# Key and value weights loaded as whole rows, first group's steps of unequal length, a normalization and some weight sums issued at other places

## The chip, the cores and the metric

The kernel runs on one core of a Trainium2 chip. The metric is the device time of one execution in microseconds (us); where several runs are shown, their median is given. Engines are named TensorE (PE in the profile, with PEld for its weight loads), VectorE (DVE), ScalarE (ACT), GpSimd (POOL) and SyncE (SP, which here only issues DMAs).

## The reference

A cross-attention block with a feed-forward block behind it, all in fp32, for 16 sequences of 128 tokens with 1024 features:

```python
x = x + xattn(layernorm(x), ctx, ctx, Wq, bq, Wk, bk, Wv, bv, Wo, bo)
x = x + ffn(layernorm(x), kernel, scale)

# xattn: 32 query heads of 32 features, 8 key/value heads, each shared by 4 query heads
Q = query @ Wq + bq            # 1024 x 1024
K = key @ Wk + bk              # 1024 x 256
V = value @ Wv + bv            # 1024 x 256
w = softmax(Q K^T / sqrt(32))  # per head, 128 x 128
y = w V
return y @ Wo + bo             # 1024 x 1024

# ffn: the last fifth of the features is weighted by -4; kernel holds zeros and ones
return scale * (concat(x[..., :819], -4 * x[..., 819:]) @ kernel)
```

The context is key and value at once, also 16 x 128 x 1024.

## The kernel before, in words

Two sequences make a group, so there are eight groups (`grp` 0 to 7). A group needs its context turned so that features lie on partitions (`cT`), keys (`prep_k`) and values (`prep_v`) from it, its normalized x turned in the same way (`prep_x`), queries (`prep_q`), attention in four steps, the output projection (`out_proj`) and the feed-forward product (`ffn`). The kernel is written so that TensorE always has dense products between the small products of attention: while group `grp` is in its four attention steps, the output projection and feed-forward of group `grp - 1` and the preparation of group `grp + 1` fill the spaces.

The order of all instructions is set by hand, by the class `Stream`. It has a model clock `now`, a queue of generators and a list of events. `piece` takes the next bit of dense work from the queue and adds its modelled length to `now`; `later(us, fn)` puts a call at a model time; `run(until)` alternates pieces with the events that are due. The model clock only orders the program: on the chip each engine takes its own instructions in program order and waits on semaphores. `mixed(dense, light, skip, every)` takes one item of `light` after every so many items of `dense`, and what is left of `light` at the end; `once(fn)` is a generator with one item of length zero; `spread(gen, us, then)` takes one step of a generator every `us`.

Attention is done in a step for each sequence and half of the heads (`attend(b, a, length)`). A step begins with 32 products of scores (`sc`, L513); at 0.7, 3.1, 5.5 and 7.9 us after them one of four blocks of heads gets its maximum on VectorE (`negm`, L525) and its exponentials on ScalarE (`p`, L529); 2.3 us later VectorE divides it (L541); and `length / 2 - 3.0` after the exponentials' event TensorE turns it (`tpp`, L546) and ScalarE copies it (`pt`, L548). At the end of the step come the products with the values (`av`, L556). `length` is 17.4 in the first group, 24.0 in groups 1 to 5 and 22.0 in group 6. PSUM tiles of `tpp`, `tp_x` (L310), `tp_f` (L646) and `av` share one pool of two buffers.

Queries and the output projection are computed with seven instead of eight block products (`seven`); for that, sums of blocks of Wq and Wo are made once by VectorE in group 0 (`combine`, L704), stored to DRAM and fetched again like the other pieces of weights through a ring of eight buffers (`fetch`, L218). `sums_of_wo` starts the sums of Wo's first half; those of the second half are started in `sums_of_wq` when Wq's second half is done. Partial results of the projection are added to the residual by VectorE straight from PSUM (L621), after which the accumulation goes on in the same PSUM tile.

The feed-forward product is made in two passes of fp32r, with a high and a low part of the turned, normalized x: `ffn_transpose` turns four chunks at a time (`tp_f`, L646), ScalarE rounds them to the high part (`x2h`, L648) and VectorE takes the difference (`x2l`, L649), after which the PSUM buffer is free.

`load_ctx` brings one sequence of context as four DMAs, each into 32 partitions: partition k * 32 + r holds rows r, r + 32, r + 64 and r + 96 of columns k * 256 to k * 256 + 255. `turn_ctx` (L319) then turns blocks of 32 x 32 on VectorE, four instructions for a group (a sequence and half of the features each). In the kernel before, chunk c of `cT` holds on partition k * 32 + f the feature k * 256 + c * 32 + f, and `load_by_quadrants` brings Wv and Wk in the same order, as four DMAs of 256 KB into 32 partitions each, alternating between SP's and ScalarE's queue.

`get_x(b, us)` loads a sequence's x (L167) and puts its normalization (`norm_x`: L276, L280, L282, the power on GpSimd at L284, L285) at `us` later. Loaded and normalized x (`xn`) and the normalized input of the feed-forward block (`x2n`) share three buffers. Residual x is loaded by `load_residual` (L172) and gets bo added by GpSimd (L178).

Of the kernel before, what the change touches and what calls it, by code (L numbers as in the profile page):

```python
# [17 lines left out]
P = 128  # L18
# [48 lines left out]
def mixed(dense, light, skip=0, every=1):  # L67


    for n, us in enumerate(dense):  # L70
        yield us
        if n >= skip and (n - skip) % every == 0:
            yield next(light, 0.0)
    yield from light


def once(fn, *args):
    fn(*args)
    yield 0.0
# [3 lines left out]
def kernel(  # L83
# [26 lines left out]
    GB = 2  # L110
# [38 lines left out]
    NB = P // 32  # L149

    def load_ctx(b, queues=(nc.sync,)):
        c_t = work.tile([P, NB, NC, 32], FP, tag="ctx", name=f"ctx{b}", bufs=2)
        src = key_value[b].rearrange("(t r) (k c f) -> k r t (c f)", r=32, k=NB, c=NC)
        for k in range(NB):
            dst = c_t[k * 32 : (k + 1) * 32].rearrange("r t c f -> r t (c f)")
            queues[k % len(queues)].dma_start(out=dst, in_=src[k])
        cs[b] = c_t

    def load_by_quadrants(dst, w, queues):
        src = w.rearrange("(k c f) n -> k f c n", k=NB, f=32)  # L160
        for k in range(NB):
            queues[k % len(queues)].dma_start(out=dst[k * 32 : (k + 1) * 32], in_=src[k])

    def load_x(b):

# [16 lines left out]

    two = (nc.sync, nc.scalar)
    load_ctx(0, two)
    load_by_quadrants(wv_sb, Wv, two)
    load_ctx(1, two)
    load_by_quadrants(wk_sb, Wk, two)
    load_x(0)
    load_x(1)
    nc.gpsimd.dma_start(out=bkT, in_=bk)  # L190
# [123 lines left out]
    def turn_ctx(b, h):  # L314
        grp, j = b // GB, b % GB
        if (grp, h) not in cTs:
            cTs[grp, h] = work.tile([P, HC, T], FP, tag="tT", name=f"cT{grp}_{h}", bufs=3)
        src = cs.pop(b) if h == 1 else cs[b]
        nc.vector.transpose(  # L319
            cTs[grp, h][:, :, j * S : (j + 1) * S].rearrange("p c (t n) -> p t c n", t=NB),  # L320
            src[:, :, h * HC : (h + 1) * HC],
        )

    def prep_ctx(grp, *us):
# [388 lines left out]
    def spread(gen, us, then=lambda: None):  # L713


        def step():
            if next(gen, "end") != "end":
                stream.later(us, step)
            else:
                then()  # L720

        stream.later(us, step)
# [14 lines left out]
    with tc.manual_schedule():  # L737
        stream = Stream()

        at_q = {}  # L740
        for k in range(2):
            for o in range(2):
                for r in range(2):
                    at_q[r, o, k] = want(lambda r=r, o=o, k=k: q_block(r, o, k))
        qs, os = {1: prep_q(1)}, {}
        for grp in range(NGRP):
            os[grp] = out_proj(grp)
            if grp + 2 < NGRP:
                qs[grp + 2] = prep_q(grp + 2)
        for _ in range(RING):  # L750
            fetch()
        o_parts = [load_o_part(0)]

        def plain(a):
            return prep_q_plain(a, {(r, k): at_q[r, a, k] for r in range(2) for k in range(2)})

        for j in range(GB):
            for h in range(2):
                turn_ctx(j, h)
            stream.add(prep_v(0, [j]))  # L760
        stream.add(prep_k(0))
        for j in range(GB):
            load_ctx(GB + j)
        stream.run(0.0, lambda: len(stream.queue) > 1)
        nc.vector.tensor_scalar_mul(bqs, bqT, scale)
        for j in range(GB):
            norm_x(j)

        def sums_of_wo():
            def then():  # L770
                o_parts.append(load_o_part(1))
                for j in range(GB):
                    load_x(GB + j)
                load_ffn()

            stream.later(4.0, lambda: spread(combine("o", 0, o_parts[0]), 1.5, then))

        stream.add(prep_x(0, 0), prep_x(0, 1), once(sums_of_wo), plain(0))
        stream.run(0.0, lambda: stream.queue)

        def get_x(b, us):
            load_x(b)
            stream.later(us, lambda: norm_x(b))

        def get_ctx(grp):
            if grp < NGRP:
                for j in range(GB):
                    load_ctx(grp * GB + j)

        def residuals(grp):  # L790
            for j in range(GB):
                load_residual(grp * GB + j, 1.0 if grp == 0 else 4.0)

        def sums_of_wq(k):
            def then():
                for _ in range(4):
                    fetch()
                if k == 1:
                    spread(combine("o", 1, o_parts[1]), 2.5)

            spread(combine("q", k, {(r, o): pieces[at_q[r, o, k]] for r, o in BLOCKS}), 1.5, then)

        def between(gen, n, fn, *args):

            for i, us in enumerate(gen):
                yield us
                if i + 1 == n:
                    fn(*args)

        for grp in range(NGRP):  # L810
            b0, b1, nxt = grp * GB, grp * GB + 1, grp + 1
            p0, p1 = b0 - 2, b0 - 1
            first, more = grp == 0, nxt < NGRP
            last = grp == NGRP - 1
            length = 17.4 if first else 24.0 if grp < NGRP - 2 else 22.0
            if first:
                stream.add(
                    once(prep_ctx, nxt, 12.5, 13.5),
                    between(plain(1), 9, sums_of_wq, 0),
                    once(sums_of_wq, 1),  # L820
                    once(turn_ctx, nxt * GB, 1),
                    once(turn_ctx, nxt * GB + 1, 1),
                    once(norm_x, nxt * GB),
                    prep_k(nxt),
                    once(get_ctx, nxt + 1),
                    once(norm_x, nxt * GB + 1),
                    prep_v(nxt),
                    prep_x(nxt, 0),
                    prep_x(nxt, 1),
                    once(convert_ffn),  # L830
                    between(qs[nxt], 40, residuals, grp),
                )
            elif more:
                stream.add(
                    once(get_x, nxt * GB, 14.0),
                    once(prep_ctx, nxt, 3.7, 8.0, 13.0, 18.0),
                    os[grp - 1],
                    once(get_ctx, nxt + 1),
                    prep_k(nxt),
                    mixed(prep_v(nxt), chain(ffn_transpose(p0), ffn_transpose(p1)), 1, 2),  # L840
                    once(get_x, nxt * GB + 1, 5.0),
                )
                if nxt < NGRP - 1:
                    stream.add(ffn(p0), mixed(ffn(p1), prep_x(nxt, 0), 12))
                else:
                    stream.add(mixed(ffn(p0), prep_x(nxt, 0), 14))
                stream.add(once(residuals, grp), prep_x(nxt, 1), qs[nxt])
            else:
                stream.add(
                    os[grp - 1],  # L850
                    mixed(ffn(p1 - 2), ffn_transpose(p0), 10, 2),
                    once(load_residual, b0, 2.0),
                    mixed(ffn(p0), ffn_transpose(p1), 8, 2),
                    once(load_residual, b1, 2.0),
                )
            if not more:
                for q in range(2 * NA):
                    b, a = grp * GB + q % GB, q // GB
                    start = stream.now
                    pts = attend(b, a, 15.0)  # L860
                    stream.later(15.0, lambda b=b, a=a, pts=pts: weighted(b, a, pts) or 1.0)
                    stream.run(start + 12.0)
                stream.drain()
                break
            for q in range(2 * NA):
                b, a = grp * GB + q % GB, q // GB
                start = stream.now
                pts = attend(b, a, length)
                if q == 2 * NA - 1:
                    stream.run(start + length - 2.0, lambda: stream.queue)  # L870
                else:
                    stream.run(start + length - 2.0)
                stream.run(stream.now, lambda: None in pts)
                weighted(b, a, pts)
                stream.now += 1.0
        stream.add(
            os[NGRP - 1],
            mixed(ffn(B - 3), ffn_transpose(B - 2), 10, 2),
            mixed(ffn(B - 2), ffn_transpose(B - 1), 8, 2),
            ffn(B - 1),  # L880
        )
        stream.drain()
# [49 lines left out]
```

## Time and profile before

| | us |
|---|---|
| median of 3 runs | 819.83 (819.57 to 819.86) |
| the profiled execution's own time | 817.83 |
| its span | 816.1 |
| TensorE busy | 789.8 (97%) |
| VectorE busy | 459.9 (56%) |
| ScalarE busy | 332.7 (41%) |
| first matmul starts | 12.29 |

Times within the profile count from the start of the span. In a timeline row the columns are: start, length, engine, line and operation, output and inputs with their shapes, number of instructions merged into the row, and in brackets how long the engine had been idle before it and what ended that. In a row of windows they are: the stretch, its length, busy time and number of instructions of each engine, the granted TensorE clock, the share of the DMA engines and the GB/s moved. Groups 1 to 5 follow one another at a distance of 97.5 us (their k products start at 153.3, 250.8, 348.4, 445.9 and 543.4).

### The profile page before, as it was taken

The page shows a single profiled execution, that of the slowest core. Times are in us where ns is not written, and L with a number is a line of the kernel's source. Part 1 is how long each engine was busy: PE and PEld are TensorE (multiplying, and loading weights), DVE is VectorE, ACT ScalarE, POOL GpSimd, SP SyncE. Part 2 cuts the span into 40 slices and gives each one's busy share as a digit, 9 for nine tenths or more (in the row PEclk, how much of TensorE's full clock was granted, in tenths as well). Part 3 has the DMA queues.
Part 4 walks back from the last instruction along what each step waited for, and adds up shares of the span by engine and source line. Part 5 has one row for each costly group of instructions (what it writes and reads, how often), then busy time and mean ns, then how long its engine had stood idle before and what let it go on. Part 6 is the DMA issues. An engine that isn't in the chain of part 4 may idle for free.

```text
span 816.1 us, 13885 instructions
## 1 busy us (share of the span) xinstructions
PE 789.8 (97%) x5216; PEld 593.4 (73%) x5216; DVE 459.9 (56%) x862; ACT 332.7 (41%) x1281; POOL 69.6 (9%) x109
## 2 busy tenths in 40 slices
PE   3997999999999999999999999999999999999998
PEld 3886884678947797488965889568894779756556
DVE  1369748554475554755456454765348565467442
ACT  0243854444334443345333544344434454366200
POOL 1000003002000020000300002000200002000300
PEclk9999999999999999999999999999999999999999
DMA  9999598715885178741887328780578307761511
GB/s 202 357 319 317 198 399 326 210 52 182 273 269 164 43 238 274 262 130 44 286 269 253 80 103 280 276 242 29 179 262 281 132 27 274 246 215 69 195 62 77
DMA packets 81075, 165.14 MB, mean 202 GB/s; under 512 B 5969, under 2 KB 42833, under 8 KB 81009
## 3 DMA queue, kind: packets, MB, share of 16 engines
q1 hardware_dynamic: 79200, 162.55, 59.6%
q10 hardware_dynamic: 1664, 1.57, 1.1%
q8 instruction: 41, 0.67, 0.3%
q0 software_dynamic: 144, 0.14, 0.1%
q14 instruction: 26, 0.20, 0.1%
HBM read 147.46 MB, written 16.78 MB: 201 GB/s over the span
## 4 chain that ended last, share of the span: by engine, by line
PE 86%; DMA 6%; DVE 3%; issue 2%; SPq 1%; ACT 1%; POOL 0%; ACTq 0%; DVEq 0%; POOLq 0%
PE o_u L607 14%; PE f L293 14%; PE q_u L396 12%; PE o_v L607 7%; PE tpp L546 6%; PE q_v L396 6%; PE k L293 5%; PE v L293 5%; PE sc L513 4%; PE av L556 4%; PE o_c L607 3%; PE q_c L396 3%; DMA wo<-in_L_xattn_Wo_dram 2%; PE tp_f L646 2%; PE tp_x L310 1%
## 5 line engine op out<-in xcount | busy, mean ns | idle before, releaser
L529 ACT ACTIVATE p<-sc,negm 128x128 f32<-128x128 f32 x512 | 181.1, 369 | 155.9 <-DVE negm L525 82.3
L548 ACT COPY pt<-tpp 128x512 f32<-128x512 f32 x128 | 74.8, 590 | 117.1 <-PE tpp L546 116.6
L525 DVE TENSOR_REDUCE negm<-sc 128x4 f32<-128x512 f32 x128 | 87.3, 683 | 39.8 <-PE sc L513 39.8
L293 PE MATMUL f<-wf_sb,x2l 128*128 128x512 f32 x256 | 106.0, 414 | 0.0
L529 ACT ACTIVATION_READ_ACCUMULATOR p<-sc,negm 128x1 f32 x512 | 105.8, 207 | 0.0
L293 PE MATMUL f<-wf_sb,x2h 128*128 128x512 f32 x256 | 101.2, 396 | 0.0
L541 DVE TENSOR_TENSOR p<-p,inv 128x512 f32<-128x512 f32 x128 | 88.6, 692 | 4.4
L546 PE MATMUL tpp<-ident,p 128*128 128x128 f32 x512 | 76.7, 273 | 6.3 <-DVE p L541 4.0
L546 PEld LDWEIGHTS tpp<-ident,p 128*128 128x128 f32 x512 | 61.7, 141 | 28.1 <-issue 20.0
L396 PE MATMUL q_u<-t,piece 128*128 128x128 f32 x672 | 81.2, 276 | 0.0
L396 PEld LDWEIGHTS q_u<-t,piece 128*128 128x128 f32 x672 | 78.0, 192 | 0.2 <-DMA piece<-q 0.2
L293 PE MATMUL v<-wv_sb,cT 128*128 128x256 f32 x256 | 62.6, 387 | 12.3 <-DMA wv_sb<-in_L_xattn_Wv_dram 12.3
L178 POOL TENSOR_TENSOR x<-x,bo_b 128x256 f32<-128x256 f32 x64 | 48.8, 795 | 180.2 <-DMA x<-in_x_dram 160.1
L293 PEld LDWEIGHTS v<-wv_sb,cT 128*128 128x128 f32 x256 | 47.5, 195 | 17.7 <-issue 12.3
L607 PE MATMUL o_u<-piece,yT 128*128 128x512 f32 x128 | 59.1, 603 | 0.0
L607 PE MATMUL o_u<-piece,s 128*128 128x512 f32 x128 | 59.0, 594 | 0.0
L607 PE MATMUL o_v<-piece,s 128*128 128x512 f32 x128 | 59.0, 594 | 0.0
L293 PE MATMUL k<-cT,wk_sb 128*128 128x256 f32 x256 | 57.0, 380 | 0.0
L293 PEld LDWEIGHTS f<-wf_sb,x2l 128*128 128x128 f32 x256 | 48.1, 188 | 11.4 <-issue 1.1
L293 PEld LDWEIGHTS f<-wf_sb,x2h 128*128 128x128 f32 x256 | 48.3, 189 | 10.0 <-issue 0.5
L293 PEld LDWEIGHTS k<-cT,wk_sb 128*128 128x128 f32 x256 | 48.5, 190 | 9.0 <-issue 2.6
L564 ACT COPY yT<-av 128x512 f32<-128x512 f32 x32 | 18.7, 585 | 88.0 <-PE av L556 88.0
(77 smaller groups left out, 949.8 us busy)
## 6 DMA issues: line engine op xcount, KB each, us to landing
piece<-o SPq DMA_DIRECT2D x64, 512.0 KB, 4.4
piece<-q SPq DMA_DIRECT2D x56, 512.0 KB, 4.4
piece<-in_L_xattn_Wq_dram SPq DMA_DIRECT2D x50, 512.0 KB, 4.8
piece<-in_L_xattn_Wo_dram SPq DMA_DIRECT2D x48, 512.0 KB, 4.5
xn<-in_x_dram SPq DMA_DIRECT2D x16, 512.0 KB, 5.4
x<-in_x_dram SPq DMA_DIRECT2D x16, 512.0 KB, 4.9
ctx<-in_ctx_dram SPq DMA_DIRECT2D x60, 128.0 KB, 5.9
out_dram<-x SPq DMA_DIRECT2D x15, 512.0 KB, 2.7
```

Of the source, the lines that this page charges most:

```text
L178: lambda cut=cut: nc.gpsimd.tensor_add(x_t[:, cut], x_t[:, cut], bo_b[:, cut]) and None,
L293: nc.tensor.matmul(mm, lhsT=lhsT, rhs=rhs, start=k == 0, stop=k == n - 1)
L396: nc.tensor.matmul(mm if part is None else mm[:, part], lhsT=lhsT, rhs=rhs, start=start and n == k == 0, stop=k == len(some) - 1, skip_gro ...
L513: nc.tensor.matmul(tiles[i][:, g], lhsT=qT[rows, g], rhs=kT[rows, a, cols], start=True, stop=True,)
L525: nc.vector.tensor_reduce(negm, tile_, AX.X, ALU.max, negate=True)
L529: nc.scalar.activation(p[:, g], tile_[:, g], AF.Exp, bias=negm[:, g : g + 1], accum_out=total[:, g : g + 1],)
L541: nc.vector.tensor_mul(p, p, inv.unsqueeze(2).to_broadcast([P, NG, S]))
L546: nc.tensor.transpose(tp[:, g], p[:, g], ident)
L548: nc.scalar.copy(pt, tp)
L556: nc.tensor.matmul(mm[i * HD : (i + 1) * HD], lhsT=vs[b][:, h * HD : (h + 1) * HD], rhs=pts[i], start=True, stop=True,)
L564: nc.scalar.copy(yTs[b, a], mm)
L607: nc.tensor.matmul(mm, lhsT=lhsT[:, 2 * k + c], rhs=w[:, c], start=start and k == c == 0, stop=k == c == 1, skip_group_check=True,)
```

## The change

Four things are changed together.

1. Chunk c of the turned context now holds on partition p the feature p * 8 + c. Wv and Wk are therefore loaded with eight whole rows to a partition, each as one DMA into 128 partitions on SP's queue. The DMAs of the context stay as they are (the same bytes go to the same places); only its transposes read every eighth word instead of 32 neighbouring ones.
2. In group 0 the four attention steps get the lengths 17.4, 22.4, 16.0 and 14.0 instead of four times 17.4.
3. The sums of Wo's second half start 8 us later on the model clock, and their steps are 3.0 apart instead of 2.5; the first sum thus comes at 11 instead of 2.5 us, the stores at 23 instead of 12.5.
4. In groups 1 to 6 the loading of the next group's second x stands between the transposes of the two feed-forward inputs, as an item of `mixed`, instead of behind both.

```diff
     def load_ctx(b, queues=(nc.sync,)):
-        c_t = work.tile([P, NB, NC, 32], FP, tag="ctx", name=f"ctx{b}", bufs=2)
-        src = key_value[b].rearrange("(t r) (k c f) -> k r t (c f)", r=32, k=NB, c=NC)
+        c_t = work.tile([P, NB, 32, NC], FP, tag="ctx", name=f"ctx{b}", bufs=2)
+        src = key_value[b].rearrange("(t r) (k n) -> k r t n", r=32, k=NB)
         for k in range(NB):
-            dst = c_t[k * 32 : (k + 1) * 32].rearrange("r t c f -> r t (c f)")
+            dst = c_t[k * 32 : (k + 1) * 32].rearrange("r t f c -> r t (f c)")
             queues[k % len(queues)].dma_start(out=dst, in_=src[k])
         cs[b] = c_t
-
-    def load_by_quadrants(dst, w, queues):
-        src = w.rearrange("(k c f) n -> k f c n", k=NB, f=32)
-        for k in range(NB):
-            queues[k % len(queues)].dma_start(out=dst[k * 32 : (k + 1) * 32], in_=src[k])
...
     load_ctx(0, two)
-    load_by_quadrants(wv_sb, Wv, two)
+    nc.sync.dma_start(out=wv_sb, in_=Wv.rearrange("(p c) n -> p c n", p=P))
     load_ctx(1, two)
-    load_by_quadrants(wk_sb, Wk, two)
+    nc.sync.dma_start(out=wk_sb, in_=Wk.rearrange("(p c) n -> p c n", p=P))
...
             cTs[grp, h][:, :, j * S : (j + 1) * S].rearrange("p c (t n) -> p t c n", t=NB),
-            src[:, :, h * HC : (h + 1) * HC],
+            src[:, :, :, h * HC : (h + 1) * HC].rearrange("p t f c -> p t c f"),
...
                 if k == 1:
-                    spread(combine("o", 1, o_parts[1]), 2.5)
+                    stream.later(8.0, lambda: spread(combine("o", 1, o_parts[1]), 3.0))
...
-            length = 17.4 if first else 24.0 if grp < NGRP - 2 else 22.0
+            length = 24.0 if grp < NGRP - 2 else 22.0
...
-                    mixed(prep_v(nxt), chain(ffn_transpose(p0), ffn_transpose(p1)), 1, 2),
-                    once(get_x, nxt * GB + 1, 5.0),
+                    mixed(
+                        prep_v(nxt),
+                        chain(
+                            ffn_transpose(p0),
+                            once(get_x, nxt * GB + 1, 5.0),
+                            ffn_transpose(p1),
+                        ),
+                        1,
+                        2,
+                    ),
...
                 start = stream.now
+                if first:
+
+                    length = (17.4, 22.4, 16.0, 14.0)[q]
                 pts = attend(b, a, length)
```

## Prediction

> **What bounds the kernel now.** I read the page first, then TensorE's timeline for its pauses, then VectorE's timeline around each pause, then DMA rates by window.
>
> ```profile
> span 816.1 us, 13885 instructions
> PE 789.8 (97%) x5216; PEld 593.4 (73%) x5216; DVE 459.9 (56%) x862; ACT 332.7 (41%) x1281; POOL 69.6 (9%) x109
> 12.29 8.64 PE L293 MATMUL v<-wv_sb,cT 128*128 128x256 f32 x32 [12.29 <-DMA wv_sb<-in_L_xattn_Wv_dram]
> 46.64 7.17 PE L293 MATMUL q<-xT,piece 128*128 128x256 f32 x32 [1.04 <-DVE qT L387]
> 72.45 0.63 PE L546 MATMUL tpp<-ident,p 128*128 128x128 f32 x4 [0.77 <-ACT p L529]
> 76.27 0.63 PE L546 MATMUL tpp<-ident,p 128*128 128x128 f32 x4 [0.60 <-DVE p L541]
> 81.99 0.63 PE L546 MATMUL tpp<-ident,p 128*128 128x128 f32 x4 [3.37 <-DVE p L541]
> 669.13 0.66 PE L310 MATMUL tp_x<-ident,xn 128*128 128x128 f32 x4 [0.71 <-ACT pt L548]
> 671.13 1.06 PE L310 MATMUL tp_x<-ident,xn 128*128 128x128 f32 x8 [0.88 <-DVE inv L540]
> ```
>
> TensorE is the bound: besides the first 12.29 us its only sizeable pauses are those above and 1.37 us at 749.7. From 103 to 668 us it never stops, and groups 1 to 5 repeat every 97.5 us. So the change can gain only in the first 103 us and near 670; between them any new wait is paid in full.
>
> ```profile
> 2.00:12.00 10.00, 0.00 (x0) 0.00 (x0) 1.30 (x2) 0.00 (x0) 1.89 (x5) 1.00 1.10 204
> 19.00:22.00 3.00, 3.00 (x15) 2.65 (x15) 1.03 (x4) 0.00 (x0) 0.00 (x0) 1.00 1.02 407
> 40.00:44.00 4.00, 3.68 (x18) 2.92 (x17) 0.90 (x3) 0.37 (x1) 0.00 (x0) 1.00 1.08 195
> 60.87 1.30 DVE L319 STREAM_TRANSPOSE cT<-ctx 128x512 f32<-128x512 f32 x2
> 64.72 1.30 DVE L319 STREAM_TRANSPOSE cT<-ctx 128x512 f32<-128x512 f32 x2
> 81.16 0.69 DVE L541 TENSOR_TENSOR p<-p,inv 128x512 f32<-128x512 f32 x1
> ```
>
> The last figure of a window is GB/s. Loads into 32 partitions run at about 200 (weights and context from 2 us; context alone from 40 us, through SP only, so the second queue isn't the cause); loads into 128 partitions (x, from 19 us) at 407.
>
> **The change part by part** (gains negative).
>
> *Weights in whole rows.* Wv leaves its 32-partition form. From the first packets at 2.0 us: context 0, 0.52 MB at 204 GB/s, 2.6 us; Wv, 1.05 MB at 407, 2.6 us; context 1's half from ScalarE's queue and bv_b interleave, 0.3 to 1.6 us; 0.3 us to landing. That is 7.8 to 9.1, and I take 8.5. The first v matmul then starts near 8.6, not 12.29: -3.7. SP gives up two issues for Wv and two for Wk (0.46 us each where the queue was free) and takes one for each, which I put at 0.33 to 0.92 (bo_b's issue into 128 partitions took 0.33); ScalarE's queue loses four. None of them is on the path, since the data take longer. Next in line is context 1, some 2 us behind Wv plus its transposes, about 12 to 13; v of batch 0 covers it (first seven matmul records at the slow start, 5.1 us in all, so until 13.7). Wk then takes 2.6 us and is in by 13.5, wanted at 17.2; x by 16.
>
> *Everything behind on SP.* x and the Wq pieces start some 5.7 us earlier (2.1 MB at 407 instead of 204 saves 5.1 us, and the rest is queueing), TensorE 3.7 earlier. So Wo's first half, whose landing holds VectorE until 43.83 and through it TensorE (0.32 at 40.8, 1.04 at 46.6), gains 2 us on it; both pauses go: -1.3.
>
> *Transposes read at a stride.* Each L319 now reads its 32 features 8 words (32 bytes) apart. The trace has no strided VectorE row. The nearest is L319 itself, 0.69 us, about 0.62 from one to the next. [...] so 1.22 us each, +0.53. [...] keep 0 and 0.9 as ends. No reason allows a gain here.
> Group 0: VectorE is busy 24.3 of the 26.4 us from 58.6 to 85, four transposes lie in that stretch, and p of step 1's third head (81.16) comes out of it: 4 x 0.53 = +2.1 us there.
> Groups 1 to 6: below.
>
> ```profile
> 239.26 0.68 DVE L621 TENSOR_TENSOR x<-o_v,x 128x512 f32<-128x512 f32 x1
> 241.50 3.60 PE L607 MATMUL o_v<-piece,s 128*128 128x512 f32 x8
> ```
>
> Three transposes precede this read without a usable pause, and the PSUM tile that it frees is written again at 241.50. Slack 241.50 - 239.95 = 1.55, less 0.1 for the hand-over = 1.45. With 3 x 0.53 = 1.59 TensorE waits 0.14 there, and with it all of the products queued behind: x 6 = +0.8. The fourth transpose has 9 us until k.
>
> *Unequal steps.* Step 1 of group 0 is 22.4, so its transposes of p come 2.5 us later in the order, behind more of v. By my count of pieces the third one stands behind all of v, at 79.2 instead of 78.6 with the earlier pauses gone (74.0 and 77.0 instead of 72.45 and 76.27). It is ready at 81.99: a pause of 2.8 with unchanged transposes, 4.9 with slow ones, against 0.77 + 0.60 + 3.37 = 4.74 now: +0.2. Steps 2 and 3 shrink to 16 and 14: p's distance falls by 0.7 and 1.7, against slacks now of 2.1 or more (p written 101.36, used 103.48) and 2.3.
>
> *Sums of Wo's second half.* Eight VectorE instructions of 0.69 (now 83.5 to 89.6) and four stores on SP (now 98.1 to 101.7) move about 10 us down the model clock, out of the full stretch into step 2. VectorE pauses there 3.4 us between 92 and 103, so they fit, but a pair of 1.3 us ahead of a p can eat the slack of step 2: +0.5. Last transposes now directly precede av in both steps: +0.4 (av took 1.45 and 1.84 in steps 2 and 3, 1.07 elsewhere). The stores pass three pieces of q-sums on SP, whose 0.32 us pause at 102.5 goes: -0.3. Behind the stores wait Wo pieces and residual x; DMA is idle from 87 to 92 now and q begins earlier, which covers the 3.6 us of issuing. If that cover fails, x comes late for POOL's additions and o_u's read at 128.7 waits. Together +0.6.
>
> *Loading x earlier.* The SP load already starts when the first batch's transposes free its buffer (263.41), so it isn't moved in time; its normalization is issued 2.6 us earlier on VectorE and POOL, and there negm of the next step waits 2.2 us, harmless with 9 us before its transpose. In group 6 tp_x loses its waits of 0.71, 0.88 and 0.24, less some delay to p: -1.3. But the empty item takes a slot of `mixed`, and two transposes of the second batch now stand together, with av soon behind:
>
> ```profile
> 267.54 0.60 PE L646 MATMUL tp_f<-ident,x2n 128*128 128x128 f32 x4
> 268.54 1.07 PE L556 MATMUL av<-pt,v 128*32 128x512 f32 x8
> 268.80 0.69 DVE L649 TENSOR_TENSOR x2l<-tp_f,x2h 128x512 fp32r<-128x512 f32 x1 [0.63 <-ACT x2h L648]
> ```
>
> From a tp_f to the end of its x2l is 268.80 + 0.69 - 267.54 = 1.95 us. There are two tp buffers. Now av uses the one of a tp_f at 265.38. Then the pair stands at 267.10 and 267.54, and av wants the buffer of 267.10, free at 269.05 plus hand-over, with its place at 268.54: +0.53. Behind av on TensorE stand the next step's scores, and the copy to yT waits too; all of it only moves along. In groups 1 to 5 (same phase): +2.7. In group 6 the pair comes 6 us after av, so no wait.
>
> Sum: -3.7 -1.3 +0.2 +0.6 +0.8 -1.3 +2.7 = -2.0. The profiled execution took 817.83 (span 816.1 and 1.7 around it), so 815.8 by its own time. The median of the three runs is 819.83, 2.0 above it; so 817.8.
>
> **Rivals.**
> A, strided reads cost nothing: step 1 gives 2.8 - 4.7 = -1.9 instead of +0.2, and o_v's wait goes (-0.8): -4.9, 814.9. For it: VectorE rows of fp32 take 0.69 whatever they do, so reading isn't visibly their limit. [...]
> B, slower: VectorE becomes the bound at o_v's read. With d more per transpose the sum is -4.9 + 4d + 6 x (3d - 1.45): step 1 pays each of four, six groups pay what exceeds their slack. It passes zero at d = 0.62, a transpose of about 1.3 us; at d = 0.9 it is +6.2, 826.0. [...] Against: nothing in the trace reads that slowly.
> C, the change doesn't do what it says at the start: interleaved with context packets, Wv is also held to 204 GB/s. Then 1.97 MB end at 11.6, v starts at 11.8 or so and gains 0.5 instead of 3.7: +1.2, 821.0. [...] Against: loads into 128 partitions elsewhere run at 400.
>
> **How the numbers follow.** Forecast 0.45 (own range 816.0 to 819.5), A 0.27, B 0.18, C 0.10. 0.2% is 1.6 us, about what a measurement of this kernel can tell from no change. Faster by more: 0.6 of the forecast, nearly all of A, 0.53. Slower by more: nearly all of B, a third of C, 0.20. Same: 0.27. The range 813.8 to 821.2 reaches below A by 1 us for the start's own spread (7.8 to 9.1) and takes in C; it leaves out most of B and little else.
>
> **What would show it.** First v near 8.6; no pause before q at 46; L319's mean in VectorE's groups (0.69 = A, 1.2 = forecast, above 1.3 = B); a pause before av of 0.5 us about every 97.5 us, released by x2l; perhaps 0.1 before o_v; step 1's third tpp waiting 3 to 5 us; none at tp_x near 665. I am wrong if v starts after 11, if groups 1 to 5 stay at 97.5 us each (then the av wait isn't there), or if they grow beyond 98.3.

## The result, and the profile after

Five runs of the changed kernel gave a median of 823.46 us (822.49 to 825.38), five of the kernel before beside them 819.57. The ratio is 1.0053, 95% interval 1.0037 to 1.0069: slower by 3.9 us, where 817.8 was forecast. The profiled execution took 822.97 us by its own time, 5.14 more than that of before; its span is 5.0 longer.

These 5.14 us exceed the 3.9 between the medians, probably because the profile of before has a mean granted clock of 1.000, while 79 of the 99 executions of that kernel beside the later comparisons have 0.998 or less, which is what half clock for 3.4 us makes of 816.

The head of the page, and TensorE's pauses over 0.25 us after the start (timeline; where a pause comes in every group, once; that of group 7 is named below):

```profile
span 821.1 us, 13874 instructions
PE 791.9 (96%) x5216; PEld 594.8 (72%) x5216; DVE 471.1 (57%) x862; ACT 333.4 (41%) x1281; POOL 69.7 (8%) x109
...
11.93 2.47 PE L288 MATMUL v<-wv_sb,cT 128*128 128x256 f32 x5 [11.93 <-DMA wv_sb<-in_L_xattn_Wv_dram]
...
66.12 5.45 PE L288 MATMUL k<-cT,wk_sb 128*128 128x256 f32 x24 [1.15 <-DVE cT L314]
71.83 2.86 PE L288 MATMUL v<-wv_sb,cT 128*128 128x256 f32 x12 [0.27 <-ACT kT L344]
77.38 1.99 PE L288 MATMUL v<-wv_sb,cT 128*128 128x256 f32 x8 [1.39 <-ACT kT L344]
83.21 0.66 PE L541 MATMUL tpp<-ident,p 128*128 128x128 f32 x4 [1.67 <-ACT pt L543]
120.93 0.63 PE L541 MATMUL tpp<-ident,p 128*128 128x128 f32 x4 [0.84 <-DVE p L536]
170.95 1.06 PE L551 MATMUL av<-pt,v 128*32 128x512 f32 x8 [0.49 <-DVE x2l L644]
674.24 0.66 PE L541 MATMUL tpp<-ident,p 128*128 128x128 f32 x4 [3.68 <-ACT pt L543]
```

The wait of v is nearly as long as before. Those of q at 46 and of tp_x at 669 and 671 are gone. The wait of av stands in each of groups 1 to 5, and a pause of 3.68 us in group 6 is new. The pause at 756 in group 7 is still 1.37.

The scores open every attention step with the same 32 products in both kernels, so their starts are milestones. After minus before:

| scores of | before | after | difference | this stretch |
|---|---|---|---|---|
| group 0, second step | 63.41 | 61.87 | -1.54 | start: -1.54 |
| group 1, first step | 123.83 | 123.21 | -0.62 | group 0: +0.92 |
| group 6, third step | 654.44 | 656.60 | +2.16 | groups 1 to 5: +2.78 |
| group 6, fourth step | 678.96 | 684.18 | +5.22 | one step of group 6: +3.06 |
| group 7, last step | 742.18 | 747.40 | +5.22 | the rest: 0 |

The loss is in two places, then, and the larger lies in one step of group 6. Windows of the changed kernel there and at the start:

```profile
2.00:12.00 10.00, 0.07 (x1) 0.10 (x1) 2.06 (x2) 1.28 (x1) 1.89 (x5) 1.00 0.90 271
...
674.80:678.20 3.40, 3.40 (x16) 2.75 (x16) 1.44 (x2) 1.76 (x3) 0.00 (x0) 0.50 0.25 95
```

The start loads at 271 GB/s instead of 204. Behind the pause of 3.68 us the granted TensorE clock is 0.50 for 3.4 us. The profile of before has no such stretch.

What leads to that pause is read on VectorE and then on ScalarE. First VectorE's timeline of the changed kernel, then that of the kernel before at the same place:

```profile
667.60 1.28 DVE L271 BATCH_NORM_STATS2 st_a<-xn 128x6 f32<-128x512 f32 x2
...
670.04 0.81 DVE L280 TENSOR_SCALAR xn<-xn,mv_a,rs_a 128x1024 f32<-128x1024 f32 x1 [0.73 <-POOL rs_a L279]
670.77 0.74 DVE L655 SCALAR_TENSOR_TENSOR x<-f,fscale,x 128x512 f32<-128x512 f32 x1
671.43 0.68 DVE L520 TENSOR_REDUCE negm<-sc 128x4 f32<-128x512 f32 x1
```

```profile
666.32 0.68 DVE L525 TENSOR_REDUCE negm<-sc 128x4 f32<-128x512 f32 x1
666.92 0.17 DVE L540 RECIPROCAL inv<-total 128x4 f32<-128x4 f32 x1
667.12 0.69 DVE L541 TENSOR_TENSOR p<-p,inv 128x512 f32<-128x512 f32 x1
667.73 1.28 DVE L276 BATCH_NORM_STATS2 st_a<-xn 128x6 f32<-128x512 f32 x2
```

Before, the step's last negm (666.32) preceded the normalization of x. Now the whole normalization (667.60 to 670.85, a wait of 0.73 for GpSimd in it) and an output sum precede it, and negm comes at 671.43. ScalarE's timeline of the changed kernel shows who waits for that:

```profile
672.21 0.37 ACT L524 ACTIVATE p<-sc,negm 128x128 f32<-128x128 f32 x1 [3.73 <-DVE inv L535]
...
673.59 0.59 ACT L543 COPY pt<-tpp 128x512 f32<-128x512 f32 x1
674.05 0.62 ACT L306 COPY xT<-tp_x 128x512 f32<-128x512 f32 x1
```

The exponentials wait 3.73 us. They read negm, which ends at 672.11, 0.10 before they start; the bracket names inv because it is the last VectorE instruction that ended before them. The two copies stand behind the exponentials in ScalarE's order. What they copy TensorE had made long before:

```profile
667.66 0.60 PE L541 MATMUL tpp<-ident,p 128*128 128x128 f32 x4
...
669.96 0.60 PE L305 MATMUL tp_x<-ident,xn 128*128 128x128 f32 x4
```

These two results fill both PSUM buffers of the pool. The copy to pt frees the first of them at 674.18, and TensorE's next transposition starts at 674.24.

### The profile page after: what moved, and what is told of

It is laid out like the page before. It is cut to its first block, busy times and chain, and to the rows that moved or that the text cites. A ratio compares the mean times of both kernels' runs of the same rounds, so it can differ in the third digit from the quotient of the medians.

```text
span 821.1 us, 13874 instructions
## 1 busy us (share of the span) xinstructions
PE 791.9 (96%) x5216; PEld 594.8 (72%) x5216; DVE 471.1 (57%) x862; ACT 333.4 (41%) x1281; POOL 69.7 (8%) x109
## 4 chain that ended last, share of the span: by engine, by line
PE 91%; DVE 3%; ACT 2%; issue 2%; DMA 1%; POOL 0%; SPq 0%; DVEq 0%; POOLq 0%; ACTq 0%
PE o_u L602 14%; PE f L288 13%; PE q_u L391 12%; PE o_v L602 7%; PE tpp L541 7%; PE v L288 6%; PE q_v L391 6%; PE k L288 6%; PE sc L508 4%; PE av L551 4%; PE o_c L602 3%; PE q_c L391 3%; PE q L288 3%; PE tp_x L305 2%; PE tp_f L641 1%
```

## Experiments

**The load of x, put back and alone.** The first kernel is the changed one with only the load of x in its old place; the second is the kernel before with only that load moved (the same edit the other way round).

```diff
-                    mixed(
-                        prep_v(nxt),
-                        chain(
-                            ffn_transpose(p0),
-                            once(get_x, nxt * GB + 1, 5.0),
-                            ffn_transpose(p1),
-                        ),
-                        1,
-                        2,
-                    ),
+                    mixed(prep_v(nxt), chain(ffn_transpose(p0), ffn_transpose(p1)), 1, 2),
+                    once(get_x, nxt * GB + 1, 5.0),
```

> Changed kernel with the load of the second x back behind both feed-forward inputs' transposes; rows, steps and Wo sums stay as changed. Theory M (the moved load cost it: five av waits of 0.50 us, and in group 6 a pause of 3.7 us plus 3.4 us at half clock behind it): no wait before av, tp_x waits of group 6 as before (1.8 us in sum), 819.0, some 0.6 below the kernel before. Rival R (the strided transposes, 1.10 instead of 0.70 us, cost it): it stays 3 us or more above the kernel before, since they are still there.

> Kernel before with only the load of the second x moved between the transposes. M: av waits of 0.50 us in groups 1 to 5 (98.1 us apart instead of 97.5, +2.8) and the pause of group 6 (+3.0): 825.3. R: no more than 0.5 us from the kernel before, since its transposes are contiguous.

Put back: 816.29 us against 819.82, ratio 0.9959 (0.9945 to 0.9972). Alone: 824.98, ratio 1.0063 (1.0048 to 1.0078). So one part of four turns a gain of 3.5 us into a loss. TensorE's timeline with the load put back, group 6:

```profile
666.32 0.66 PE L305 MATMUL tp_x<-ident,xn 128*128 128x128 f32 x4 [0.72 <-ACT pt L543]
668.31 1.06 PE L305 MATMUL tp_x<-ident,xn 128*128 128x128 f32 x8 [0.87 <-DVE inv L535]
```

and with the load moved alone, its timeline in groups 1 and 6 and a window:

```profile
171.65 1.07 PE L556 MATMUL av<-pt,v 128*32 128x512 f32 x8 [0.50 <-DVE x2l L649]
674.98 1.11 PE L546 MATMUL tpp<-ident,p 128*128 128x128 f32 x4 [3.68 <-ACT pt L548]
...
675.00:681.80 6.80, 6.80 (x34) 6.14 (x35) 2.52 (x4) 3.34 (x6) 0.00 (x0) 0.56 0.47 157
```

The first has the waits of before, and from group 1 to the end its distance from before, by the scores' starts, stays at 2.8 us (within 0.04). The second has both new waits without any other part of the change, and its half clock lasts 6.8 us. From the third to the fourth step of group 6 it loses 4.25 us.

**Whole rows alone, unequal steps and late sums alone.** The kernel before with the loads of Wv and Wk and the strided transposes; and the kernel before with the four lengths and the sums of Wo's second half put off.

```diff
-    load_by_quadrants(wv_sb, Wv, two)
+    nc.sync.dma_start(out=wv_sb, in_=Wv.rearrange("(p c) n -> p c n", p=P))
...
-            src[:, :, h * HC : (h + 1) * HC],
+            src[:, :, :, h * HC : (h + 1) * HC].rearrange("p t f c -> p t c f"),
```

```diff
-                    spread(combine("o", 1, o_parts[1]), 2.5)
+                    stream.later(8.0, lambda: spread(combine("o", 1, o_parts[1]), 3.0))
...
+                    length = (17.4, 22.4, 16.0, 14.0)[q]
```

> Kernel before with only whole-row weights and strided transposes. First v near 11.9, no pauses before q at 40 to 47 (-1.4 to -1.8), step 1 of group 0 waits longer by up to 4 x 0.40 = 1.6 us. M: within 0.5 us of the kernel before, steady groups 97.5 us apart. R: 3 us or more slower, with waits before o_v in every group.

> Kernel before with only the unequal steps of group 0 and Wo's second sums put off. M and R alike: step 1's waits fall from 4.7 to about 3 us as forecast with contiguous transposes, step 3 has a pause of 0.8 us before its last transpose of p: 818.6, 1 us faster. If the prediction's count of pieces was wrong, step 1 waits as much as before and it is not faster.

Rows alone: 818.30, ratio 0.9982 (0.9969 to 0.9995). Steps and sums alone: 817.61, ratio 0.9976 (0.9966 to 0.9985). TensorE's timeline with rows alone:

```profile
9.73 9.41 PE L288 MATMUL v<-wv_sb,cT 128*128 128x256 f32 x32 [9.73 <-DMA wv_sb<-in_L_xattn_Wv_dram]
64.16 5.45 PE L288 MATMUL k<-cT,wk_sb 128*128 128x256 f32 x24 [1.14 <-DVE cT L314]
80.07 1.09 PE L541 MATMUL tpp<-ident,p 128*128 128x128 f32 x4 [3.36 <-DVE p L536]
```

v starts 2.56 us earlier than before, and the second step's scores 3.48. In group 0 of this profile more than that is lost again: k waits for the slower transposes, the pause before the third tpp is still 3.36, and half clock lasts 6.8 us from 79.19 on. At group 1 it stands 0.78 behind the profile of before. Groups 1 to 5 stay at 97.5 us, so slower transposes cost nothing there. With steps and sums alone, the pauses over 0.25 us in step 1 are 1.46 and 1.68 instead of 4.74 in all.

**The two costs of the early load, one at a time.** Both kernels keep the load early. The first calls it inside the run of transposes without an item of its own in `mixed`; the second keeps the item and puts the normalization at 7.6 instead of 5.0.

```diff
-                            ffn_transpose(p0),
-                            once(get_x, nxt * GB + 1, 5.0),
+                            between(ffn_transpose(p0), 2, get_x, nxt * GB + 1, 5.0),
```

```diff
-                            once(get_x, nxt * GB + 1, 5.0),
+                            once(get_x, nxt * GB + 1, 7.6),
```

> Changed kernel, but the load of the second x is called where it stands now without being an item of its own, so that it takes no slot of the mixture; its normalization stays as early as in the changed kernel. If the pair of transposes is what av waits for: no wait before av, groups 97.5 us apart, -2.8. If the early normalization causes group 6's pause: 3.7 us there and the 3.4 us or more at half clock stay, so about 820.0. If instead the pair causes both, group 6 is as in the kernel before and the time is 816.5.

> Changed kernel with the slot kept, and the normalization put 7.6 instead of 5.0 us after the load, so where the kernel before had it. Av waits of 0.50 us in groups 1 to 5 stay; group 6 loses the pause of 3.7 us and the stretch at half clock and has the waits of the kernel before (1.8 us): 816.3 + 2.8 = 819.1. If the pair causes group 6's pause, it stays, and the time is 822 or more.

Without the item: 819.12, ratio 1.0003 (0.9988 to 1.0017). With the late normalization: 819.70, ratio 0.9999 (0.9987 to 1.0011). TensorE's timeline of the first, group 6:

```profile
670.22 0.66 PE L305 MATMUL tp_x<-ident,xn 128*128 128x128 f32 x4 [3.88 <-ACT pt L543]
```

and of the second, in groups 1 and 6, with VectorE's in group 6:

```profile
171.81 1.06 PE L551 MATMUL av<-pt,v 128*32 128x512 f32 x8 [0.50 <-DVE x2l L644]
672.01 0.66 PE L541 MATMUL tpp<-ident,p 128*128 128x128 f32 x4 [0.48 <-ACT pt L543]
674.01 1.06 PE L305 MATMUL tp_x<-ident,xn 128*128 128x128 f32 x8 [0.88 <-DVE inv L535]
...
669.20 0.68 DVE L520 TENSOR_REDUCE negm<-sc 128x4 f32<-128x512 f32 x1
...
670.61 1.28 DVE L271 BATCH_NORM_STATS2 st_a<-xn 128x6 f32<-128x512 f32 x2
```

Each edit takes away its own cost and leaves the other: the first has no wait before av and groups of 97.5 us, but still loses 3.28 us in group 6; the second loses 2.87 in groups 1 to 5 and nothing in group 6. There the last negm stands ahead of the normalization again, as before, which agrees with the chain read above.

**Both at once, and the changed kernel again.** The early load without an item and with the late normalization, and the changed kernel unaltered, in one comparison.

> The changed kernel with both costs of the moved load taken away and the load still early: it takes no slot among the transposes, and its normalization comes at 7.6 instead of 5.0 us. If these two are all that the moved load costs, no wait at av, none of 3.7 us near 674, no half clock there, and the time is that of the kernel with the load in its old place: 816.3, ratio 0.996. If loading early costs something else too (the buffers that it holds, the transfer), 818 or more. If the early load also spares the waits of tp_x near 665, below 815.5.

> The changed kernel once more, beside the others of this comparison. If the parts add (rows alone -1.5, steps and sums alone -2.0, the moved load alone +5.2), it stands 1.7 us above the kernel before, ratio about 1.002, and part of the 1.0053 of its first comparison was spread of the late half-clock stretches and of the start. If the first comparison was typical, it stands 4 us above, 1.005.

Both at once: 816.87 against 819.55, ratio 0.9965 (0.9953 to 0.9977), where the load in its old place gave 0.9959. TensorE's timeline, group 6:

```profile
668.45 0.66 PE L305 MATMUL tp_x<-ident,xn 128*128 128x128 f32 x4 [0.71 <-ACT pt L543]
```

The waits are those of before, so within these intervals the two costs are all that the moved load brought, and the early load brings no gain of its own. The changed kernel again: 822.53, ratio 1.0040 (1.0026 to 1.0055). Its profiled execution started v at 9.69 instead of 11.93 and was ahead of before by 3.93 us at the second step, yet lost 2.84 in groups 1 to 5 and 3.21 in group 6. The sum of the parts, 1.7 us by their ratios (-1.5 for rows, -2.0 for steps and sums, +5.2 for the load), is below this interval's 2.1 to 4.5; the parts' own intervals of about a microsecond each cover the difference, so the parts may simply add, but an effect of one on another is not excluded.

**The start.** The changed kernel with the load of x in its old place, and Wv's transfer left alone: context 1 all on SP behind Wv, GpSimd's four small loads issued by SP behind Wk.

```diff
-    load_ctx(1, two)
+    load_ctx(1)
...
+    nc.sync.dma_start(out=bkT, in_=bk)
...
-    nc.gpsimd.dma_start(out=bkT, in_=bk)
...
```

> Version with the load of x back, and at the start nothing beside Wv on other queues: all of context 1 behind Wv on SP, and GpSimd's four small loads (bk, bv, bq, scale) issued by SP behind Wk. If interleaving holds Wv's slowest engine up: landing by 8.5, first v at 8.6 (the prediction's start), and if everything behind follows, 815. If the spread over the sixteen engines is there anyway: v at 9.7 to 11.9 as in the runs so far, 816.3.

815.54, ratio 0.9951 (0.9934 to 0.9967), not distinguishable from 0.9959. Its TensorE timeline:

```profile
11.58 4.91 PE L288 MATMUL v<-wv_sb,cT 128*128 128x256 f32 x11 [11.58 <-DMA wv_sb<-in_L_xattn_Wv_dram]
```

v starts late although nothing interleaves. For Wv's DMA the trace records sixteen completions, one for each part, and v starts 0.14 us behind the last. Fifteen came by 8.32 here, as the forecast of 8.5 had it, and the last at 11.44; in the changed kernel's first profile fifteen came by 9.77 and the last at 11.79. In the ten profiles with the context beside Wv the fifteenth came at 9.18 to 10.51 (median 9.68), the last at most 0.6 us behind it in eight and 1.9 and 2.0 us in two. So two delays add up: one late part, which is seen in some profiles, with the context or without, and about 1.4 us for all parts beside the context, though only one profile without it supports that figure. Why a part is late was not settled.

**The waits of tp_x.** The changed kernel with the load of x in its old place and the transposes of x put further apart, `mixed(ffn(p0), prep_x(nxt, 0), 20)` for 14.

> Version with the load of x back, and in group 6 the transposes of the next x put behind all pieces of the feed-forward product (the number of pieces ahead of them 20 instead of 14). Theory: tp_x waits for the normalization on VectorE and the copy on ScalarE, which end at 671 whatever TensorE does; one piece of 0.47 us moves ahead of them, so 0.5 of the 1.8 us goes: 815.8. Rival: the copies behind it wait in the same order and nothing changes.

815.82, ratio 0.9959 (0.9945 to 0.9973): the waits are 0.24, 1.34 and 0.24 instead of 0.72, 0.87 and 0.24. They only change places.

**Steps and sums apart.** Both with the load in its old place and whole rows: the first with the sums of Wo's second half not put off, the second with four steps of 17.4.

> The load in its old place, whole rows and unequal steps kept, the sums of Wo's second half not put off. If putting them off is what makes room on VectorE for the slower transposes, step 1's p comes late again: pauses of 2 us more there, 818 to 819. If the unequal lengths alone do it, 816.3 as with the sums put off.

> The load in its old place, whole rows and the sums put off kept, the first group's four steps of 17.4 each. If the longer step 1 is what gives p its distance, the third tpp of step 1 waits 3 us again as with whole rows alone, and 818 or more. If putting the sums off is enough, 816.3; if the shorter steps 2 and 3 cost more than step 1 gains, below 815.5.

Sums not put off: 818.17, ratio 0.9982 (0.9973 to 0.9992). Equal steps: 818.92, ratio 0.9983 (0.9970 to 0.9996). TensorE's timeline of the first, then of the second:

```profile
112.43 2.92 PE L391 MATMUL q_v<-xT,piece 128*128 128x128 f32 x24 [0.77 <-DMA piece<-q]
```

```profile
72.73 0.63 PE L541 MATMUL tpp<-ident,p 128*128 128x128 f32 x4 [0.93 <-ACT p L524]
76.55 0.63 PE L541 MATMUL tpp<-ident,p 128*128 128x128 f32 x4 [0.60 <-DVE p L536]
82.27 1.09 PE L541 MATMUL tpp<-ident,p 128*128 128x128 f32 x4 [3.36 <-DVE p L536]
```

Against 816.29 and 816.87 of the kernels that have both, each is worth 1.3 to 2.6 us by the medians; the intervals of the ratios still touch. They don't work by one mechanism. Putting the sums off does nothing for step 1, whose pauses stay the same (1.16, 0.27, 1.39, 1.67); it keeps their stores away from the q-sums, whose wait of 0.77 at 112 comes back without it (group 0 is 1.2 us longer in that profile; the rest was not traced). The longer step is what shortens the pause of 3.36.

## Why the prediction was wrong

Of the 7.2 us between the forecast of -2.0 and the measured +5.22, 4.4 lie in group 6 and 3.5 in the start; the wait at o_v's read, which did not come, takes 0.8 off.

**Group 6, the failed step.** "In group 6 tp_x loses its waits of 0.71, 0.88 and 0.24, less some delay to p: -1.3" measured +3.06 (3.21 in the second profile). Those waits do go, but the "2.2 us" by which negm waits was called harmless from groups 1 to 5, "with 9 us before its transpose", and carried into group 6. There the normalization takes 3.25 us of VectorE, and what counts is not the transposition of this p: it is the copy of an earlier tpp that ScalarE has queued behind the exponentials of this negm. That queue was not followed. In group 2 the delayed negm (272.68) is the first of its step, and ScalarE has no tpp to copy until 283.08; in group 6 it is the last of its step, with a copy already due. One new pause of 3.68 replaces 0.71 + 0.88 + 0.24 = 1.83, which makes +1.85. The half clock adds 1.2.

That 1.2 is from group 0. Eight profiles, two of them of the changed kernel itself, have group 0 with the changed order in full. In four of them a half clock of 3.4 us follows the pauses of step 1, and the stretch from the second step's scores to group 1 costs 2.07 to 2.11 against before; in the other four it costs 0.91 to 0.93. So 1.17 for 3.4 us, and 1.85 + 1.2 = 3.05 for the measured 3.06. With 6.8 us of it, in the kernel with only the load moved, 1.85 + 2.4 = 4.25, as measured.

When half clock comes can be read from the records of the granted clock. In all fourteen profiles the changes of the clock after the start lie whole multiples of 3.413 us apart (193 between the start of full clock and the half clock of group 6, 20 to that of group 0), so each execution has a grid of intervals. These are two of them in group 0, each with the one behind it, first in the changed kernel and then in that with the late normalization:

```profile
80.89:84.30 3.41, 1.74 (x11) 1.05 (x10) 2.51 (x7) 2.81 (x11) 0.00 (x0) 1.00 0.83 336
84.30:87.72 3.42, 2.99 (x25) 2.56 (x25) 1.18 (x2) 2.91 (x7) 0.00 (x0) 1.00 0.01 4
...
81.28:84.70 3.42, 1.58 (x12) 1.26 (x12) 1.82 (x5) 3.10 (x11) 0.00 (x0) 1.00 0.70 287
84.70:88.11 3.41, 3.41 (x18) 3.00 (x17) 1.35 (x3) 2.12 (x4) 0.00 (x0) 0.50 0.00 0
```

Of the intervals at full clock in the fourteen profiles, half clock followed all 15 in which TensorE was busy for 1.22 us or less, four of the five with 1.51 to 1.58, and none with 1.60 or more. It lasted for 6.8 us where TensorE paused again in the first 3.4 (2.52 and 2.53 busy). Busy times are modelled, so the boundary is a rough one. The pauses of 3.6 to 3.9 us in group 6 always left an interval with 0.63 or less. The pause of 3.37 before the third tpp fell across two intervals of the profile of before (1.86 and 1.60 busy) and stayed without half clock; with whole rows alone it left one with 0.94. So the same pauses cost 1.2 us or nothing here, by where they fell on the grid.

**The start, mis-sized.** "-3.7" and "-1.3" together forecast -5.0 at the second step; measured -1.54, in the second profile -3.93, and the median of the eleven profiled kernels with whole rows is -2.75. The pauses before q at 40.8 and 46.6 went as forecast (-1.36). The landing failed: v at 8.6 was forecast, the eleven show 9.65 to 11.93, median 10.45. Two terms of the sum were too small. The context beside Wv was allowed 0.3 to 1.6 us, with a landing at 8.5, but fifteen of the sixteen parts were there only at a median of 9.68. And bytes over rate leaves out the last part, 2.0 us later in the changed kernel's first profile. Rival C named the time (11.8) but not the cause: the window shows 271 GB/s, not 204, and the last part of the undisturbed Wv was just as late. Part of an early start is given back, too: full clock was granted 3 to 6 us after the first product (3.0 before, 4.1 in the changed kernel), and until then a product of v took 0.63 to 0.77 us, afterwards 0.38.

**The wait before av, right.** Forecast +0.53 in each of groups 1 to 5, +2.7 in all; measured 0.49 to 0.50 at av, +2.78 in all, released by x2l, and gone when the item is.

**The strided transposes, nearly right.** The row of L314, by tile (minimum, median, maximum in ns), and the o_v read of group 2 on VectorE with TensorE's use of the tile behind it:

```profile
L314 DVE STREAM_TRANSPOSE cT<-ctx x32: 1049/1098/1114, 5.5 to 633.4; 128x512 f32<-128x512 f32 x32
...
240.40 0.68 DVE L616 TENSOR_TENSOR x<-o_v,x 128x512 f32<-128x512 f32 x1
...
241.44 3.60 PE L602 MATMUL o_v<-piece,s 128*128 128x512 f32 x8
```

They take 1.10 us, +0.40 against 0.70 (the same row before: 668/702/711 ns). The forecast's 1.22, +0.53, was the author's estimate; the trace of before had no row that could show it. Three of them cost 1.2 us, below the slack of 1.45 (the hand-over in it, put at 0.1, took 0.05 to 0.15 at the pauses of before, from the end of VectorE's or ScalarE's instruction to TensorE's start), so the "+0.8" for o_v's read is 0: o_v is read at 240.40 + 0.68 and used at 241.44 without a pause. Rival A's price (0) and rival B's (1.3 and more) are both excluded.

**Group 0, right in sum, in part by luck.** "+0.2" for step 1 and "+0.6" for steps and sums: forecast +0.8, measured +0.92, but 2.1 in the four of eight profiles that have half clock there. The size of step 1's pauses is right (4.9 forecast; 1.15 + 0.27 + 1.39 + 1.67 + 0.24 + 0.19 = 4.91), their places are not. One pause of 4.9 before the third tpp was expected; there are four larger ones, one behind a transpose (cT), two behind ScalarE's copies of kT and one behind its pt.

With what was measured the sum is -1.54 + 0.92 + 2.78 + 3.06 = +5.22 against the forecast of -2.0, and the profiled executions differ by 5.14.

A version that beats both kernels is the changed one with the load of x in its old place: 816.29, ratio 0.9959.

## What to carry to other kernels

Before an instruction is moved up in one queue, follow what it delays through the queues behind it, stage by stage: here VectorE's negm held ScalarE's exponentials, those held an unrelated copy, and the copy held a PSUM buffer. A slack read in one group did not hold in a group whose steps have another length and another filling. A transfer that everything waits for is to be sized by its last part (1.9 to 3.1 us behind the other fifteen in three of eleven loads of Wv), and a pause on TensorE by its own length and the half clock that may follow (1.2 us behind the pause of 3.68). A forecast that starts from one profile should ask first whether that execution is a typical one.

## What was not expected of the hardware

- Half clock came in stretches of 3.4 or 6.8 us, at 1.2 us of time for each 3.4, on a grid of 3.413 us, behind intervals in which TensorE was busy for 1.58 us or less. Pauses of 1.39 and 1.67 us a few microseconds apart were enough in four of eight profiles: the same order of group 0 cost 2.07 to 2.11 us with it and 0.91 to 0.93 without.
- A load of 1 MB into 128 partitions landed 7.9 to 10.1 us after its issue in eleven profiles of the same DMA; in three of them the last of its sixteen parts came 1.9 to 3.1 us after the other fifteen.
- A VectorE transpose of 128 x 512 fp32 in blocks of 32 x 32 took 1.10 us (median of 32) with 32 bytes between its elements and 0.70 with neighbouring ones.
